# Layer 0, first pair of a two-layer directional scan: the upward scan's rows kept whole in DRAM, stored in 512-byte runs and loaded by columns in 128-byte runs

## The chip, the cores and the metric

The kernel runs on one core of a Trainium2 chip. The metric is device microseconds of one execution. All numbers are float32.

## The reference

A tensor x of 32 images, 48 channels, 64 rows and 128 columns goes through two layers. Each layer normalizes x by groups of three channels and then runs four scans, one after the other, over rows and then over columns; in each, a line becomes its own value plus a 5-tap convolution of the line before it.

```python
def _conv1d(x, w, b):                     # 48 -> 48 channels, 5 taps along the line
    y = conv_general_dilated(x, w, window_strides=(1,), padding=[(2, 2)], ...)
    return y + b[None, :, None]
def step(w, b):
    def f(carry, inp):
        nxt = inp + _conv1d(carry, w, b)
        return (nxt, nxt)
    return f
D = scan(step(down_w, down_b))  over rows 0..63
U = scan(step(down_w, down_b))  over D's rows 63..0
R = scan(step(right_w, right_b)) over U's columns 0..127
L = scan(step(left_w, left_b))  over R's columns 127..0
...
x = x + layer0(_gn(x));  x = x + layer1(_gn(x))      # _gn: group norm, 16 groups
```

A scan is serial: step n needs the line of step n-1. A row scan has 63 steps, a column scan 127.

## The kernel before

**Phases.** The 32 images are four groups of eight. `PHASES` sets the order: in layer 0, the rows of group 0, 1, 2 and 3 (phases 0 to 3, each a down scan and an up scan), then the columns of the first pair (groups 0 and 1, phase 4, a right scan and a left scan) and of the second pair (groups 2 and 3, phase 5); then the same for layer 1. The page names a step's PSUM tile `step_01d` for layer 0, group 1, down; `u` is up, and `step_00r` and `step_00l` are the right and left scans of layer 0, first pair. One step is 18 matmul records on TensorE (nine products, each split in two passes) and three `scalar_tensor_tensor` on VectorE (L913), one for each third of the partitions. VectorE's instruction of a step reads the PSUM sum, the bias and the line's own value, and writes the new line in place of that value; the next step's matmuls read it.

**Layouts.** In a row phase a partition holds one (column modulo 8, channel), 384 of them in three parts of 128, and its free axis holds the rows one after the other: a row is 128 floats, 16 columns by 8 images, 512 bytes. In a column phase a partition holds one (row modulo 8, channel); a quarter of the columns (`quarter`, j = 0 to 3) is six units of 128 x 2048 floats, 8 KB in a partition. Between the two the data go through DRAM. The tensors `upa` (one for each group, layer 0) keep the up scan's rows, `xin` keeps the input turned into the row layout, and `mid` the result of layer 0.

**Buffers.** `arena` has three slots of 48 KB in a partition and a stage of four units. A row phase takes two slots (rows 0 to 31 and rows 32 to 63), a column phase three: quarters 0, 1 and 2 lie in the three slots, and quarter 3 takes the place of quarter 0 after that has been spilled to DRAM.

**Queues.** Nearly all transfers of layer 0 are issued by SyncE (SP on the page) in program order (L288 for all, the helper `dma`). A DMA uses one of eight semaphores in turn, so a new one waits until the eighth before it has landed. `PIECES` cuts a block of 384 partitions into ten pieces of 48, 32 or 16 partitions: a block of eight rows is ten DMAs, a quarter of columns of two groups is twenty. What SP issues in phases 0 to 3, by the page's names:

- `arena<-in_x`: a part of the raw input of a later group, 2 MB, in six pieces for a group (`take_in`);
- `xin<-arena`: that input after GpSimd has turned it (L699, `permute`), 1 KB runs (`put_out`);
- `arena<-xin`: the rows of the next phase, in four loads of 16 rows, twenty DMAs each, 128-byte runs (`move_rows` with `to_dram` false);
- `upa<-arena`: the rows of an up scan, in eight stores of eight rows, ten DMAs each, 128-byte runs (`move_rows` with `to_dram` true, through `by_row`);
- `arena<-upa`: the quarters of the column phase, runs of 8 KB, one for each partition (`load_unit`, through `by_col`).

**Order.** `plan_rows`, `plan_cols` and `plan_input` give each piece of side work a time in steps, and all engines' instructions are written out in that order. For a row phase that starts at step t0, `plan_rows` puts the loads of rows 0, 16, 32 and 48 at t0-36, -26, 0 and +11 (phase 1: -34, -18, -3 and +12) and their scaling on ScalarE (L777, `scale_rows`, 24 instructions for 16 rows) at t0-18, -8, +16 and +30 (phase 1: -12, -2, +17 and +33). The stores of an up scan that starts at t_up stand at t_up+12, 20, 28 and 36 for rows 56 to 32, and for rows 24 to 0 at 30, 42, 54 and 66 steps into the next phase. `plan_input` puts the statistics of a later group's input on ScalarE between them (L570 and L562, `take_others`), one batch for each of the six `in_x` pieces; phase 1 does group 2's, phase 2 group 3's. After the sixth batch, VectorE makes the group's scale from them (L587 to L603) among the steps of the up scan. `plan_cols` loads quarter 0 at 54 to 44 steps ahead of the column phase, quarter 1 at 24 to 14 ahead, quarter 2 at 8 to 18 behind its start, the spill of quarter 0 at 33 to 43 and quarter 3 at 50 to 60.

The functions that the change touches and those that call them, with the line numbers of the profile:

Of the kernel before, what the change touches and what calls it, by code (L numbers as in the profile page):

```python
# [42 lines left out]
E8 = 8  # L43
FULL = 128
NG = E8 * C // FULL
NQ = 4
# [68 lines left out]
    ("cols", 1, 1),  # L115
)
JOINED = (8, 9)


@with_exitstack  # L120
def kernel(
# [11 lines left out]
    NH = H // E8  # L133
# [3 lines left out]
    RUN = KQ * GB  # L137
# [89 lines left out]
    def by_row(t, e, h0, h1):  # L227


        t = t.rearrange("c (i q a e n) -> e a c i q n", i=E8, q=NQ, a=NH, e=E8)[e, h0 // E8]  # L230
        t = t[:, h0 % E8 : h0 % E8 + h1 - h0]
        return t.rearrange("c i q n -> c (i q) n")

    def x_by_row(t, e, h0, h1):

        t = t.rearrange("(i q) c (a e n) -> e a c i q n", i=E8, a=NH, e=E8)[e, h0 // E8]
        return t[:, h0 % E8 : h0 % E8 + h1 - h0].rearrange("c i q n -> c (i q) n")
# [44 lines left out]
    def by_col(t, e, j):  # L282


        return t.rearrange("c (i q n) -> i q c n", i=E8, q=NQ)[e, j]

    def dma(dst, src, queue=None):
        (queue or nc.sync).dma_start(dst, src)  # L288
# [21 lines left out]
    def pieces(o):  # L310
        return [(e, c0, c1, p0) for e, c0, c1, g, p0 in PIECES if g == o]
# [404 lines left out]
    def place(k, h):  # L716


        first = k
        while first in JOINED:  # L720
            first -= 1
# [5 lines left out]
    def rows_at(k, h0, h1):  # L727

        places = sorted(place(k, h) for h in range(h0, h1, E8))
        at = places[0] * E8 + h0 % E8  # L730
        assert h0 // HALF == (h1 - 1) // HALF and places[-1] - places[0] == len(places) - 1
        return row_views(k)[h0 // HALF][:, :, at : at + h1 - h0]
# [4 lines left out]
    def move_rows(k, h0, h1, to_dram):  # L737

        _, layer, g = PHASES[k]
        t = (ups if to_dram else source)[layer][g]  # L740
        for h in range(h0, h1, E8):
            end = min(h1, h + E8)
            view = rows_at(k, h, end)
            for o in range(NG):
                for e, c0, c1, p0 in pieces(o):
                    here = view[p0 : p0 + c1 - c0, o]
                    here = here.rearrange("p h (q n) -> p (h q) n", q=NQ)
                    if to_dram:
                        dma(by_row(t, e, h, end)[c0:c1], here)
                    else:  # L750
                        dma(here, (x_by_row if g else natural_row)(t, e, h, end)[c0:c1])
# [41 lines left out]
    def quarter(k, j):  # L793
        return slot[slots(k)[j % 3]].rearrange("p (o s n) -> p s o n", s=2, o=NG)

    def load_unit(k, j, i):


        _, layer, pair = PHASES[k]
        o, half = UNITS[i]  # L800
        unit = quarter(k, j)[:, half, o]
        t = ups[layer][2 * pair + half]
        for e, c0, c1, p0 in pieces(o):
            here = unit[p0 : p0 + c1 - c0]
            dma(here, by_col(t, e, j)[c0:c1])

    def spill_unit(k, i, back):
        _, layer, pair = PHASES[k]
# [134 lines left out]
    def two_row_step(ku, hu, kd, hd):  # L943

        _, layer, g = PHASES[ku]
        first = slots(ku)[0] < slots(kd)[0]

        def both(u, d, o):
            u, d = lines(u[:, o]), lines(d[:, o])
            return beside(*((u, d) if first else (d, u)))  # L950

        def inp(o):
            if hu:
                return both(row(ku, hu - 1), row(kd, hd), o)
            pair = lines(last.rearrange("p (o n) -> p o n", o=NG)[:, o]), lines(row(kd, hd)[:, o])
            return pair if first else pair[::-1]

        def part(t, s):
            return t[:, max(0, s) : NK + min(0, s)]

        step(
            f"{layer}{g}u{hu}d{hd}",
            wt[f"down{layer}"],
            (layer, DOWN),
            lambda i: both(row(ku, hu + 1), row(kd, hd - 1), i),
            inp,
            lambda o: both(row(ku, hu), row(kd, hd), o),
            lambda ps: ps.rearrange("p (c q m b) -> p c q m b", c=2, q=NQ, b=GB),
            part,
            lambda t: t.rearrange("p c q m b -> p (q m) c b"),  # L970
        )
# [27 lines left out]
    def scans(k):  # L999
        if PHASES[k][0] == "rows":  # L1000
            if k not in JOINED:
                for h in range(1, H):
                    yield 1, lambda h=h: row_step(k, h, row(k, h - 1), row(k, h), "d")
            end = last.rearrange("p (o n) -> p o n", o=NG)
            for h in range(H - 2, -1, -1):
                if k + 1 in JOINED:
                    yield 2, lambda h=h: two_row_step(k, h, k + 1, H - 1 - h)
# [13 lines left out]
    def at(t, fn, *args):  # L1021
        agenda.append((t, len(agenda), fn, args))
# [31 lines left out]
    def plan_rows(k, t0, prev):  # L1054
        layer = PHASES[k][1]
        down, up = (2 if k in JOINED else 1), (2 if k + 1 in JOINED else 1)
        t_up = t0 + down * (H - 1)
# [4 lines left out]
        else:  # L1062
            ahead, scaled = (-54, -43, 0, 11), (-22, -8, 16, 30)
            if not PHASES[k][1]:
                ahead, scaled = (-36, -26, 0, 11), (-18, -8, 16, 30)
        if k in JOINED:
            for i in range(H // E8):
                h, t = i * E8, t0 + 2 * i * E8
                for o in range(NG):
                    at(t - 34 + 2 * o, take_rows, k, h, h + E8, o)  # L1070
                at(t - 17, scale_rows, k, h, h + E8)
        elif k:
            for i in range(4):
                if PHASES[k][1]:
                    for o in range(NG):
                        t = t0 + ahead[i] - 2 + 3 * o
                        at(t, take_rows, k, i * LOAD, (i + 1) * LOAD, o)
                else:
                    at(t0 + ahead[i], move_rows, k, i * LOAD, (i + 1) * LOAD, False)
                at(t0 + scaled[i], scale_rows, k, i * LOAD, (i + 1) * LOAD)  # L1080

        following = PHASES[k + 1][0] == "cols"
        for i in range(H // E8):
            h0 = H - E8 * (i + 1)
            t = t_up + up * (H - 1 - h0)
            if up == 2:
                t += 1
            elif not following and not layer:
                t = t_up + 12 + 8 * i if i < 4 else t_up + H - 1 + 30 + 12 * (i - 4)
            elif not following:  # L1090
                t = t_up + 29 + 5 * i + (34 if i >= 4 else 0)
            at(t, move_rows, k, h0, h0 + E8, True)
# [7 lines left out]
    def plan_cols(k, t0, prev):  # L1100
# [3 lines left out]
        for i in range(n):  # L1104
            early = 30 if after else 58 if k - 1 in JOINED else 54
            at(t0 - early + 2 * i, load_unit, k, 0, i)
            at(t0 + (3 if after else -24 + 2 * i), load_unit, k, 1, i)
            at(t0 + (38 if after else 8) + 2 * i, load_unit, k, 2, i)
            at(t0 + 33 + 2 * i, spill_unit, k, i, False)
            at(t0 + 50 + 2 * i, load_unit, k, 3, i)  # L1110
# [77 lines left out]
    starts, end = [], 0  # L1188
    for k, (kind, *_) in enumerate(PHASES):
        n = (H if kind == "rows" else W) - 1  # L1190
        starts.append(end - 2 * n if k in JOINED else end)
        end = starts[-1] + (2 if k in JOINED else 1) * n + (2 if k + 1 in JOINED else 1) * n
# [28 lines left out]
    def first_group():  # L1221
# [163 lines left out]
        scale_at_once(0, 2, 4, nc.vector)  # L1385
        put_rows(pool, act, pool)
        move_rows(0, 8, 12, False)
        put_rows(pool, act, pool, act, pool, act)
        scale_shared(8, 12)
# [84 lines left out]
```

## Time and profile before

| | us |
|---|---|
| median of 3 runs | 4126.9 (4126.24 to 4131.73) |
| profiled execution, its own time | 4129.7 |
| its span, first to last instruction | 4128.0 |
| TensorE busy | 4015.7 |
| VectorE busy | 2082.2 |
| ScalarE busy | 1307.0 |
| GpSimd busy | 789.3 |

The profiled execution lies 2.8 us above the median. TensorE's step starts place the phases, in us from the span's start: phase 0 down 61.3 and up 198.7; phase 1 down 324.5 and up 457.7; phase 2 down 586.8 and up 718.2; phase 3 down 845.7 and up 970.2; phase 4 right 1094.6 and left 1343.0; phase 5 from 1591.3; layer 1 from 2090.9. A row of the windows view gives a stretch of time, the busy time of each engine in it with its number of instructions, then the granted TensorE clock, the mean busy share of the 16 DMA engines and the GB/s that they moved. A row of the timeline gives the start, the length, the engine, the operation, out<-in, how many equal ones follow each other, and in brackets the idle time ahead of it and what ended that. For SP the length is the time in which it issued, not the time of the transfer.

### The profile page before, as it was taken

What the parts mean: (1) busy time and instruction counts of PE and PEld (TensorE: products, weight loads), DVE (VectorE), ACT (ScalarE), POOL (GpSimd) and SP (SyncE); (2) the same over time, 40 slices, a digit from 0 to 9 for tenths busy, and PEclk for the clock granted to TensorE, in tenths of its full rate; (3) what the DMA queues carried; (4) which work ended last, traced back from release to release, by engine and by line L of the source; (5) the groups of instructions that cost most, each with busy time, mean ns of one, the idle gap of its engine ahead of it and who ended that gap; (6) DMA issues with size and microseconds to landing.
All of it is one profiled execution on the core that took longest, in us unless ns stands there. A gap on an engine that the chain in (4) does not pass through costs nothing. (4 is left out here: it accounts for less than half of the span.)

```text
span 4128.0 us, 85199 instructions
## 1 busy us (share of the span) xinstructions
PE 4015.7 (97%) x34360; PEld 3930.1 (95%) x34360; DVE 2082.2 (50%) x6137; ACT 1307.0 (32%) x2628; POOL 789.3 (19%) x672
## 2 busy tenths in 40 slices
PE   6999999999999999999999999999999999999994
PEld 5999999999999999999999998888999999999994
DVE  6454454544444567545656443333444444444444
ACT  4556547450000256003674633434000002300122
POOL 5631303200000243002411000000000015610353
PEclk9999999999999999999999999999999999999997
DMA  9898998986990399814896965666698029999799
GB/s 300 217 203 171 222 157 211 208 132 116 165 226 1 89 261 285 210 20 151 217 171 146 141 107 95 100 108 100 100 171 205 1 70 252 294 246 157 148 233 195
DMA packets 2207818, 681.57 MB, mean 165 GB/s; under 512 B 2008848, under 2 KB 2157504, under 8 KB 2182080
## 3 DMA queue, kind: packets, MB, share of 16 engines
q1 hardware_dynamic: 2071488, 595.36, 69.7%
q10 hardware_dynamic: 135936, 80.77, 8.1%
q8 instruction: 270, 4.42, 0.5%
q14 instruction: 124, 1.02, 0.1%
HBM read 399.11 MB, written 295.93 MB: 168 GB/s over the span
## 5 line engine op out<-in xcount | busy, mean ns | idle before, releaser
L834 POOL TENSOR_TENSOR arena<-arena 128x2048 f32<-128x2048 f32 x80 | 362.5, 4548 | 1714.7 <-PE step_00l L899 499.9
L777 ACT ACTIVATE arena<-arena,offsetr,scaler 128x128 f32<-128x128 f32 (+1 forms) x576 | 345.1, 687 | 348.4 <-DMA arena<-mid 291.0
L638 ACT ACTIVATE early<-arena 128x256 f32<-128x256 f32 x192 | 129.7, 676 | 816.0 <-POOL arena L834 809.6
L777 ACT ACTIVATE arena<-arena,offset,scale 128x256 f32<-128x256 f32 (+2 forms) x360 | 248.8, 785 | 151.4 <-DMA arena<-xin 143.2
L699 POOL COPY arena<-arena 128x256 f32<-128x256 f32 x340 | 201.0, 658 | 443.1 <-DMA arena<-in_x 392.5
L899 PE MATMUL step_01r<-arena,early 128*128 128x128 f32 x2286 | 249.8, 272 | 0.0
L899 PE MATMUL step_11r<-arena,early 128*128 128x128 f32 x2286 | 249.3, 272 | 0.0
L899 PEld LDWEIGHTS step_11r<-arena,early 128*128 128x128 f32 x2286 | 248.7, 184 | 0.6 <-DVE arena L913 0.3
L899 PEld LDWEIGHTS step_01r<-arena,early 128*128 128x128 f32 x2286 | 248.9, 184 | 0.2
L899 PE MATMUL step_00r<-arena,early 128*128 128x128 f32 x2286 | 248.5, 272 | 0.0
L899 PE MATMUL step_10l<-arena,wleft 128*128 128x128 f32 x2286 | 248.5, 272 | 0.0
L899 PE MATMUL step_11l<-arena,wleft 128*128 128x128 f32 x2286 | 248.5, 272 | 0.0
L899 PE MATMUL step_10r<-arena,early 128*128 128x128 f32 x2286 | 248.5, 272 | 0.0
L899 PEld LDWEIGHTS step_00r<-arena,early 128*128 128x128 f32 x2286 | 248.5, 184 | 0.0
L899 PE MATMUL step_00l<-arena,wleft 128*128 128x128 f32 x2286 | 248.4, 272 | 0.0
L899 PE MATMUL step_01l<-arena,wleft 128*128 128x128 f32 x2286 | 248.4, 272 | 0.0
L899 PEld LDWEIGHTS step_10l<-arena,wleft 128*128 128x128 f32 x2286 | 248.4, 184 | 0.0
L899 PEld LDWEIGHTS step_11l<-arena,wleft 128*128 128x128 f32 x2286 | 248.4, 184 | 0.0
L899 PEld LDWEIGHTS step_10r<-arena,early 128*128 128x128 f32 x2286 | 248.4, 184 | 0.0
L899 PEld LDWEIGHTS step_00l<-arena,wleft 128*128 128x128 f32 x2286 | 248.4, 184 | 0.0
L899 PEld LDWEIGHTS step_01l<-arena,wleft 128*128 128x128 f32 x2286 | 248.4, 184 | 0.0
L856 ACT COPY arena<-arena 128x256 f32<-128x256 f32 x172 | 99.7, 657 | 367.1 <-POOL arena L834 241.0
(545 smaller groups left out, 6880.6 us busy)
## 6 DMA issues: line engine op xcount, KB each, us to landing
xin<-arena SPq DMA_DIRECT2D x94, 512.0 KB, 5.1
arena<-in_x SPq DMA_DIRECT2D x18, 2048.0 KB, 10.0
upa<-arena SPq DMA_DIRECT2D x192, 192.0 KB, 4.1
arena<-upa SPq DMA_DIRECT2D x96, 384.0 KB, 11.7
arena<-xin SPq DMA_DIRECT2D x96, 384.0 KB, 10.7
upb<-arena SPq DMA_DIRECT2D x192, 192.0 KB, 3.9
arena<-upb SPq DMA_DIRECT2D x96, 384.0 KB, 11.1
arena<-xin SPq DMA_DIRECT2D x174, 192.0 KB, 4.3
```

The source lines that it names most:

```text
L638: nc.scalar.activation(junk[:, 0:n], view[:, b], AF.Identity, accum_out=self.sum[:, i, j : j + 1])
L699: copy(dst[:, r, q], src[:, r0 + r, q])
L777: nc.scalar.activation(args[0], args[0], AF.Identity, bias=args[2], scale=args[1])
L834: eng.tensor_tensor(unit, unit, nat, ALU.add)
L856: copy(by_w(perm)[:, a], src[:, a])
L899: nc.tensor.matmul(part(turn(whole(ps[o]))[0:m], -s), weights[:, i, at : at + m], part(turn(src(i)), s), start=seen[o] == 1, stop=seen[o] ...
```

## The change

The DRAM tensors of layer 0's groups 0 and 1 are read as (channel, row modulo 8, row divided by 8, column modulo 8, 128 floats): the 16 columns by 8 images of one row and one column residue stand together, 512 bytes. Before, they stood in four runs of 128 bytes, one in each quarter of the columns. A store of eight rows now has 8 runs of 512 bytes for a partition in place of 32 of 128, and a load of a unit has 64 runs of 128 bytes for a partition, 512 bytes apart, in place of one of 8 KB. Groups 2 and 3 and layer 1 keep the old form.

```diff
 JOINED = (8, 9)
+WHOLE = ((0, 0), (0, 1))
...
+    def whole_row(t, e, h0, h1):
+        t = t.rearrange("c (i a e n) -> e a c i n", i=E8, a=NH, e=E8)[e, h0 // E8]
+        return t[:, h0 % E8 : h0 % E8 + h1 - h0]
...
+    def part_of_rows(t, e, j):
+        return t.rearrange("c (i m q n) -> i q c m n", i=E8, q=NQ, n=RUN)[e, j]
...
                 for e, c0, c1, p0 in pieces(o):
                     here = view[p0 : p0 + c1 - c0, o]
+                    if to_dram and (layer, g) in WHOLE:
+                        dma(whole_row(t, e, h, end)[c0:c1], here)
+                        continue
                     here = here.rearrange("p h (q n) -> p (h q) n", q=NQ)
...
-            dma(here, by_col(t, e, j)[c0:c1])
+            if (layer, 2 * pair + half) in WHOLE:
+                dma(here.rearrange("p (m n) -> p m n", n=RUN), part_of_rows(t, e, j)[c0:c1])
+            else:
+                dma(here, by_col(t, e, j)[c0:c1])
```

Of 320 stores to `upa` 160 change their form, and of 160 loads from it 80. No instruction is added, removed or moved on any engine. A row of SP's list gives its number, the line, out<-in and the sizes of the destination: partitions, runs, floats of a run. The first store of group 0's up scan read before:

```order
78 L288 DMA upa_88<-arena 48x32x32 x2
79 L288 DMA upa_88<-arena 32x32x32
80 L288 DMA upa_88<-arena 16x32x32
81 L288 DMA upa_88<-arena 48x32x32 x2
82 L288 DMA upa_88<-arena 16x32x32
```

and now (the helper `dma` has moved from L288 to L298):

```order
78 L298 DMA upa_88<-arena 48x8x128 x2
79 L298 DMA upa_88<-arena 32x8x128
80 L298 DMA upa_88<-arena 16x8x128
81 L298 DMA upa_88<-arena 48x8x128 x2
82 L298 DMA upa_88<-arena 16x8x128
```

Nothing moved: a partition's eight rows go out in 8 runs of 128 floats, where they went in 32 runs of 32. The first loads of phase 4 on the same list read before:

```order
520 L288 DMA arena<-upa_88 48x2048 x2
521 L288 DMA arena<-upa_88 32x2048
522 L288 DMA arena<-upa_89 48x2048 x2
523 L288 DMA arena<-upa_89 32x2048
524 L288 DMA arena<-upa_88 16x2048
```

and now:

```order
520 L298 DMA arena<-upa_88 48x64x32 x2
521 L298 DMA arena<-upa_88 32x64x32
522 L298 DMA arena<-upa_89 48x64x32 x2
523 L298 DMA arena<-upa_89 32x64x32
524 L298 DMA arena<-upa_88 16x64x32
```

They stand at the same places, and a partition's unit comes in 64 runs of 32 floats, where it came in one of 2048.

## Prediction

> **What bounds the kernel now.** I read the waits of TensorE first, since a chain of serial steps ends when TensorE's last step ends; each row gives who waited for whom, us in total, times, longest.
>
> ```profile
> PE step_01d L899 <- DVE arena L913: 6.8, 1, 6.8
> PE step_02d L899 <- DVE arena L913: 5.4, 1, 5.4
> PE step_01u L899 <- DVE arena L913: 2.8, 3, 1.5
> PE step_02u L899 <- DVE arena L913: 1.5, 2, 1.3
> ```
>
> Apart from the first 170 us, which the change doesn't reach, TensorE waits in phases 1 and 2 and nowhere else for more than a fraction of a microsecond. The windows view, cut at the starts of the scans (phase 0 up; 1 down, up; 2 down, up; 3 down, up), prices it.
>
> ```profile
> 198.70:324.50 125.80, 125.55 (x1144) 125.36 (x1143) 63.81 (x211) 65.63 (x144) 40.41 (x69) 1.00 0.95 205
> 324.50:457.70 133.20, 126.36 (x1136) 126.17 (x1136) 60.73 (x190) 88.85 (x173) 32.17 (x55) 0.97 0.84 189
> 457.70:586.80 129.10, 126.33 (x1145) 125.76 (x1145) 65.48 (x211) 52.39 (x116) 25.46 (x44) 1.00 0.96 192
> 586.80:718.20 131.40, 126.00 (x1136) 125.81 (x1135) 60.64 (x189) 93.91 (x180) 31.43 (x54) 0.99 0.90 198
> 718.20:845.70 127.50, 125.95 (x1144) 125.57 (x1144) 65.84 (x211) 52.76 (x116) 27.88 (x46) 1.00 0.98 195
> 845.70:970.20 124.50, 124.50 (x1137) 124.50 (x1137) 60.57 (x190) 53.82 (x72) 0.00 (x0) 1.00 0.74 116
> 970.20:1094.60 124.40, 124.40 (x1136) 124.40 (x1135) 60.64 (x189) 0.00 (x0) 0.50 (x1) 1.00 0.89 150
> ```
>
> A quiet down scan takes 124.5 us (phase 3). An up scan in which VectorE also makes a group's scale takes 125.8 when nothing is late (phase 0). So phase 1 loses 8.7 and 3.3 us, phase 2 loses 6.9 and 1.7: 20.6 us in all. The granted clock is down to 0.97 and 0.99 just where TensorE stood still. Who is late is told by VectorE's and ScalarE's timelines and by the one line of source L588.
>
> ```profile
> 426.23 0.61 DVE L913 SCALAR_TENSOR_TENSOR arena<-step_01d,bd,arena 128x128 f32<-128x128 f32 x2 [7.10 <-DMA arena<-in_x]
> 655.33 0.61 DVE L913 SCALAR_TENSOR_TENSOR arena<-step_02d,bd,arena 128x128 f32<-128x128 f32 x2 [5.66 <-ACT arena L777]
> 525.16 0.21 DVE L592 TENSOR_TENSOR neg_x_x<-neg_x_x,mean_x_x 128x48 f32<-128x48 f32 x1 [2.56 <-ACT early L562]
> L588 DVE TENSOR_SCALAR mean_x_x<-mean_x_x x3: 171/1933/2222, 254.7 to 780.2; 128x8 f32<-128x8 f32 x3
> 512.11 9.48 POOL L699 COPY arena<-arena 128x256 f32<-128x256 f32 x16 [23.94 <-DMA arena<-in_x]
> ```
> ```profile
> 395.43 0.63 ACT L570 ACTIVATE early<-arena 128x512 f32<-128x512 f32 x1 [9.83 <-DMA arena<-in_x]
> 408.37 17.83 ACT L777 ACTIVATE arena<-arena,offset,scale 128x256 f32<-128x256 f32 x24
> 624.52 0.63 ACT L570 ACTIVATE early<-arena 128x512 f32<-128x512 f32 x1 [18.71 <-DMA arena<-in_x]
> 637.47 17.84 ACT L777 ACTIVATE arena<-arena,offset,scale 128x256 f32<-128x256 f32 x24
> ```
>
> VectorE stood 7.10 us ahead of row 48 of phase 1 and went on at 426.23, when the 24 scalings of rows 48 to 63 ended (408.37 + 17.83 = 426.20); the DMA named there landed long before. These scalings stand behind a batch of statistics, and that batch began when its piece of `in_x` landed (395.43). At 655.33 it is the same chain one batch earlier: `in_x`, statistics, rows 32 to 47. At 525.16 VectorE itself waits for the last batch. And L588, 0.17 us when alone, took 1.93 while GpSimd's copies ran to 521.59. All four are one lateness, that of the `in_x` pieces, and SP's timeline tells where they stand.
>
> ```profile
> 225.20 10.23 SPq L288 DMA_DIRECT2D upa<-arena  x10
> 239.83 12.74 SPq L288 DMA_DIRECT2D upa<-arena  x10
> 256.42 12.52 SPq L288 DMA_DIRECT2D upa<-arena  x10
> 289.89 11.10 SPq L288 DMA_DIRECT2D upa<-arena  x10
> 301.04 43.97 SPq L288 DMA_DIRECT2D arena<-xin  x40
> 345.06 0.98 SPq L288 DMA_DIRECT2D arena<-in_x  x1
> 383.94 1.00 SPq L288 DMA_DIRECT2D arena<-in_x  x1
> 615.07 1.31 SPq L288 DMA_DIRECT2D arena<-in_x  x1
> 616.43 26.27 SPq L288 DMA_DIRECT2D arena<-xin  x20
> ```
>
> SP issues without a pause from 225 to 346: four stores of group 0, then sixty row loads, then `in_x`. The queue is the bound there, not the step that a plan gives a transfer.
>
> **The stores.** Their price is read from stretches in which one kind of transfer runs (last two columns: busy share of the DMA engines, GB/s).
>
> ```profile
> 209.00:224.00 15.00, 15.00 (x139) 15.00 (x138) 7.17 (x24) 14.36 (x39) 13.60 (x24) 1.00 0.85 296
> 227.00:235.00 8.00, 8.00 (x76) 8.00 (x75) 3.85 (x12) 7.68 (x21) 6.80 (x12) 1.00 0.96 155
> 303.00:345.00 42.00, 42.00 (x384) 42.00 (x384) 20.57 (x64) 18.18 (x25) 0.00 (x0) 1.00 0.94 144
> 1137.00:1157.00 20.00, 20.00 (x186) 20.00 (x185) 10.06 (x32) 0.00 (x0) 0.00 (x0) 1.00 1.02 194
> 1206.00:1222.00 16.00, 16.00 (x150) 16.00 (x149) 7.87 (x26) 0.00 (x0) 0.00 (x0) 1.00 1.06 218
> ```
>
> They are: 1 KB runs stored from 128 partitions; 128-byte stores; 128-byte row loads; the 8 KB column loads; 1 KB and 8 KB loads of residuals in pieces of 48, 32 and 16 partitions. A block of eight rows is 384 x 4 KB = 1.57 MB. At 155 GB/s that is 10.1 us, which is the row 10.23. No row shows runs of 512 bytes. The ends: at 296/0.85 = 348 GB/s it takes 4.5 us, with no gain 10.2; a loss I leave out, since there are four times fewer runs of the same bytes. The nearest rows are those of the same pieces with long runs, 194 and 218. I take 200 GB/s: 7.9 us, a gain of 2.3 for a block.
>
> The four stores of phase 0 put SP 4 x 2.3 = 9.2 us ahead at the loads of 301.04 and so at 345.06 and 383.94. The rows that they store are ready in time (the fourth block at 198.7 + 31 x 1.98 = 260). Then rows 48 to 63 are scaled 9.2 us earlier, and the wait of 7.10 is gone by 2. The next bound there is the step itself. The eight stores between 345 and 615 give 18 more. On the way SP also waits for GpSimd and for its input buffer, which come free earlier by the same chain, so I count 20 to 27 of lead at 615.07. Phase 2 starts 8.7 + 3.3 = 12.0 earlier; its rows 32 need 12.0 + 5.66 = 17.7 of lead, its rows 48 (scaled just in time now) about 20. Both are met, the second with little to spare. With a lead of some 17 at the last batch, VectorE's 2.56 us is gone and GpSimd's copies end before L588 (521.59 - 17 against 519.7 - 8.7). In phase 2's up scan the lead is larger. So all 20.6 us come back. The price at which the first wait would remain: a block over 8.4 us.
>
> That the queue carries the same number of DMAs, ten for a block, is no new bound: ten row loads with fewer bytes are issued in less than 10 us, and the landing of eight in flight only gets quicker.
>
> **The loads.** These lie beside phases 3 and 4, whose TensorE is full. The rows: SP's issues of quarters 1 (its end), 2 and 3; the median time to landing of these 384 KB DMAs, 11.7 us; and the right scan's matmuls (first and last start).
>
> ```profile
> 1103.47 3.02 SPq L288 DMA_DIRECT2D arena<-upa  x6
> 1134.27 23.71 SPq L288 DMA_DIRECT2D arena<-upa  x20
> 1172.08 28.60 SPq L288 DMA_DIRECT2D arena<-upa  x20
> ```
> ```profile
> arena<-upa SPq DMA_DIRECT2D x96, 384.0 KB, 11.7
> ```
> ```profile
> L899 PE MATMUL step_00r<-arena,early x2286: 259/275/335, 1094.6 to 1342.9; 128*128 128x128 f32 x128, 128*96 128x112 f32 x63
> ```
>
> A step takes (1342.9 - 1094.6)/127 = 1.955 us, so quarter 1 is needed at 1094.6 + 31 steps = 1155, quarter 2 at 1218, quarter 3 at 1280. They landed at 1118, 1170 and 1212: 37, 48 and 68 us to spare. A quarter is 6.29 MB: 32.4 us at 194 GB/s. In 128-byte runs the same bytes are the forty row loads of 43.97 us, with the same partition pieces and as many runs: 44.0. Each quarter costs 11.6 more, and since DMA engines are full from 993 on, the delays add up: 23 at quarter 1, 35 at quarter 2, 46 at quarter 3. All are below what is to spare, the least by 13. The sum's term is 0; the cover is gone at a quarter of 48.4 us. The ends: 44.0, and the slowest 128-byte row loads, 26.27 for half a quarter beside a 2 MB `in_x`, 52.5: quarter 3 then lands 80 late against 68, 12 us of stall. I take 44.0, as no `in_x` runs there. Above these rows lies one thing that no row shows: runs 512 bytes apart, so that a quarter reads a fourth of each row. What is behind (residual loads, used from step 34 of the left scan) has over 100 us.
>
> Against this speaks a sum of fixed costs: 128-byte stores at 155 GB/s take 13.2 ns a run on each of 16 engines, 1 KB stores at 348 take 47.1, which leaves 8.4 ns for a run whatever its size. If that came on top of a quarter's 32.4, its 49152 runs would add 25.8 and make 58. The forty row loads are as many runs in the same pieces and took 44.0, so the two costs overlap, in those loads at least.
>
> The Trainium skill, DMA: Bandwidth & Descriptors, "Why small descriptors are slow (HBM only)", gives each packet about 3 cycles beside its 32-byte beats. By that rule, as an estimate, 64 runs of 128 bytes are 448 cycles where one of 8 KB is 259, and a quarter of 32.4 becomes 56 us, near the 58; the row of 43.97 doesn't bear it out for row loads.
>
> **Sum.** 4129.7 for the profiled execution less 20.6 is 4109.1. It stood 2.8 above the median, so 4126.9 - 20.6 = 4106.3 for the median.
>
> **Rivals.** First, a part only: a block costs over 8.4 us, say 9.2. Lead 4 at 383.94: phase 1 keeps 3 of its 7 us, phase 2's rows 48 some of theirs; 10 to 14 us come back, about 4115. For it: the stores stand among 1 KB stores (12.74, 12.52), where I priced them alone. Against: 194 and 218 in the same pieces.
>
> Second, slower: the cost of a run adds to the pace of the pieces, 58 us a quarter. That is 25.4 over the present; quarter 3 lands 102 later against 68 to spare, 34 us of stall, 4140. The point from which this decides: 20.6 = 4 x excess - 68, an excess of 22, a quarter of 54.6 us. Against it the 144 GB/s of the row loads, which would have to fall to 108. The skill's rule above would give 56 us and 4133.
>
> Third, slower too, by another cause: runs 512 bytes apart load at well under the row loads' rate. The long runs of these column loads go at 194 where 348 is seen elsewhere; the same fall would make 79 us of 44. Half way, 62 us: quarter 3 is 4 x 29.6 = 118 late, 50 of stall, 4157. Against: the fall is seen with residuals from another tensor (218), so it belongs to the pieces, which the 43.97 has already.
>
> Fourth, 512-byte runs gain nothing and the loads are hidden: 4127.
>
> **Chances.** All back: 0.63. A part: 0.16. Costs that add: 0.07. Runs apart: 0.06. Nothing: 0.08. Faster by over 0.2% (8.3 us, about what a measurement here can tell) is all back and nearly all of the part, 0.77; within 0.2% the nothing and the tail of the part, 0.10; slower 0.13. The range: the low end is the whole excess of phases 1 and 2 over phase 3 (8.7 + 4.7 + 6.9 + 3.1 = 23.4), with no cost of the scale left: 4103. The high end takes in the part: 4121. Left out are both slower ones and most of the nothing.
>
> **What would show it.** Right: no wait of TensorE over 2 us in phases 1 and 2; down scans of 124 to 126 us; the four stores under 9 us each; `in_x` issued near 336; quarter loads of twenty at about 44 us and none awaited; phase 4 at 248.3. Wrong: stores of 10 us, a new wait in `step_00r` near its steps 32, 64 or 96, or rows still scaled late because statistics and not SP set the pace.

## Result: 21.7 us faster, and the profile after

On one chip the kernel before took 4129.31 us (median of 4, 4126.24 to 4132.28), the changed one 4107.58 (median of 4, 4105.10 to 4109.53): a ratio of 0.9947 [0.9930, 0.9964], a gain of 15 to 29 us by its interval. The profiled execution of the changed kernel took 4108.49 of its own, its span is 4106.8, 21.2 below the 4128.0 of before. The line numbers have moved: `dma` is L298, TensorE's step L915, VectorE's L929, the statistics L580, the scaling L790.

The waits of TensorE after, from phase 0's up scan to phase 3 (us in total, times, longest). There are no others in these scans; `step_01d` and `step_02d` are gone from the list.

```profile
PE step_02u L915 <- DVE arena L929: 0.3, 1, 0.3
PE step_00u L915 <- DVE arena L929: 0.3, 1, 0.3
PE step_01u L915 <- DVE arena L929: 0.3, 1, 0.3
```

The windows after, cut again at the starts of the scans (phase 0 up; 1 down, up; 2 down, up; the last row is phase 4 right):

```profile
198.20:324.00 125.80, 125.55 (x1144) 125.36 (x1143) 63.87 (x211) 79.04 (x162) 40.34 (x69) 1.00 0.94 220
324.00:448.50 124.50, 124.50 (x1136) 124.50 (x1136) 60.60 (x190) 85.11 (x179) 38.27 (x65) 1.00 0.80 211
448.50:574.40 125.90, 125.65 (x1144) 125.46 (x1144) 63.91 (x211) 61.70 (x117) 19.52 (x33) 1.00 0.91 203
574.40:698.90 124.50, 124.50 (x1137) 124.50 (x1137) 60.62 (x190) 89.14 (x190) 37.93 (x64) 1.00 0.84 230
698.90:824.80 125.90, 125.64 (x1145) 125.45 (x1144) 63.96 (x211) 57.63 (x107) 21.38 (x35) 1.00 0.91 169
1073.60:1322.30 248.70, 248.70 (x2288) 248.47 (x2288) 122.30 (x382) 0.00 (x0) 0.00 (x0) 1.00 0.86 131
```

The four scans lost 8.7, 3.2, 6.9 and 1.6 us (133.2, 129.1, 131.4 and 127.5 before), 20.4 together, and each is now within 0.1 us of the length that a quiet scan of its kind had before (124.5 down, 125.8 up). The granted clock is 1.00 in all of them. Phase 4's right scan, in which the loads are slower, kept its length (248.7 here, 248.4 before, from 1094.6 to 1343.0).

SP's timeline after, rows 1 to 4 the four stores of group 0's up scan, then the row loads, the `in_x` pieces and the quarters of phase 4:

```profile
224.79 7.30 SPq L298 DMA_DIRECT2D upa<-arena  x10
236.07 9.23 SPq L298 DMA_DIRECT2D upa<-arena  x10
249.28 9.48 SPq L298 DMA_DIRECT2D upa<-arena  x10
279.10 7.84 SPq L298 DMA_DIRECT2D upa<-arena  x10
286.99 44.39 SPq L298 DMA_DIRECT2D arena<-xin  x40
331.44 0.63 SPq L298 DMA_DIRECT2D arena<-in_x  x1
370.15 0.87 SPq L298 DMA_DIRECT2D arena<-in_x  x1
576.09 0.83 SPq L298 DMA_DIRECT2D arena<-in_x  x1
1102.37 12.92 SPq L298 DMA_DIRECT2D arena<-upa  x6
1137.25 44.10 SPq L298 DMA_DIRECT2D arena<-upa  x20
1188.86 54.33 SPq L298 DMA_DIRECT2D arena<-upa  x20
```

The four stores take 33.9 us where they took 46.6, the row loads behind them are issued at the same pace as before (44.39 and 43.97), and so `in_x` is issued 13.6 us earlier. The quarters pay for it: quarter 2 was issued in 23.71 and takes 44.10, quarter 3 in 28.60 and takes 54.33.

Four rows of ScalarE's timeline after show where the lead arrives, and the line of VectorE's small scale instruction (L588 before; least, median and longest in ns) shows its stretch beside GpSimd's copies gone:

```profile
381.04 0.63 ACT L580 ACTIVATE early<-arena 128x512 f32<-128x512 f32 x1 [9.20 <-DMA arena<-in_x]
393.97 17.96 ACT L790 ACTIVATE arena<-arena,offset,scale 128x256 f32<-128x256 f32 x24
598.20 17.93 ACT L790 ACTIVATE arena<-arena,offset,scale 128x256 f32<-128x256 f32 x24
631.77 17.93 ACT L790 ACTIVATE arena<-arena,offset,scale 128x256 f32<-128x256 f32 x24
```
```profile
L598 DVE TENSOR_SCALAR mean_x_x<-mean_x_x x3: 171/171/171, 254.2 to 760.8; 128x8 f32<-128x8 f32 x3
```

Rows 48 to 63 of phase 1 are scaled at 393.97 + 17.96 = 411.9, and the step that needs them comes at 324.0 + 47 x 1.98 = 417.1: 5 us to spare where 7.1 were missing. Rows 32 to 47 of phase 2 are ready at 616.1 for a step at 574.4 + 31 x 1.98 = 635.8, and its rows 48 to 63 at 649.7 for a step at 667.5. From its issue (370.15) to the first statistic that reads it (381.04) the second `in_x` piece took 10.9 us, and 11.5 before (383.94 to 395.43): of the 14 us by which it is there earlier, the travel gives 0.6 and the issue the rest.

### The profile page after: what moved, and what is told of

It reads as the page before. It is cut to its first block, busy times and chain, and to the rows that moved or that the text cites. A ratio compares the mean times of both kernels' runs of the same rounds, so it can differ in the third digit from the quotient of the medians.

```text
span 4106.8 us, 85201 instructions
## 1 busy us (share of the span) xinstructions
PE 4012.3 (98%) x34360; PEld 3927.0 (96%) x34360; DVE 2078.8 (51%) x6137; ACT 1306.9 (32%) x2628; POOL 789.0 (19%) x672
## 5 line engine op out<-in xcount | busy, mean ns | idle before, releaser
L790 ACT ACTIVATE arena<-arena,offsetr,scaler 128x128 f32<-128x128 f32 (+1 forms) x576 | 345.2, 688 | 348.8 <-DMA arena<-mid 322.5
L790 ACT ACTIVATE arena<-arena,offset,scale 128x256 f32<-128x256 f32 (+2 forms) x360 | 249.0, 787 | 91.8 <-DMA arena<-xin 81.6
L915 PE MATMUL step_01r<-arena,early 128*128 128x128 f32 x2286 | 249.8, 272 | 0.0
L915 PE MATMUL step_11r<-arena,early 128*128 128x128 f32 x2286 | 249.2, 272 | 0.0
L915 PEld LDWEIGHTS step_11r<-arena,early 128*128 128x128 f32 x2286 | 248.7, 184 | 0.4 <-DVE arena L929 0.3
L915 PEld LDWEIGHTS step_01r<-arena,early 128*128 128x128 f32 x2286 | 248.9, 184 | 0.2
L915 PE MATMUL step_00r<-arena,early 128*128 128x128 f32 x2286 | 248.8, 272 | 0.0
L915 PEld LDWEIGHTS step_00r<-arena,early 128*128 128x128 f32 x2286 | 248.5, 184 | 0.2 <-DVE arena L929 0.2
L915 PE MATMUL step_10l<-arena,wleft 128*128 128x128 f32 x2286 | 248.5, 272 | 0.0
L915 PE MATMUL step_11l<-arena,wleft 128*128 128x128 f32 x2286 | 248.5, 272 | 0.0
L915 PE MATMUL step_00l<-arena,wleft 128*128 128x128 f32 x2286 | 248.4, 272 | 0.0
L915 PE MATMUL step_01l<-arena,wleft 128*128 128x128 f32 x2286 | 248.4, 272 | 0.0
L915 PE MATMUL step_10r<-arena,early 128*128 128x128 f32 x2286 | 248.4, 272 | 0.0
L915 PEld LDWEIGHTS step_10l<-arena,wleft 128*128 128x128 f32 x2286 | 248.4, 184 | 0.0
L915 PEld LDWEIGHTS step_11l<-arena,wleft 128*128 128x128 f32 x2286 | 248.4, 184 | 0.0
L915 PEld LDWEIGHTS step_00l<-arena,wleft 128*128 128x128 f32 x2286 | 248.4, 184 | 0.0
L915 PEld LDWEIGHTS step_01l<-arena,wleft 128*128 128x128 f32 x2286 | 248.4, 184 | 0.0
L915 PEld LDWEIGHTS step_10r<-arena,early 128*128 128x128 f32 x2286 | 248.4, 184 | 0.0
## 6 DMA issues: line engine op xcount, KB each, us to landing
arena<-in_x SPq DMA_DIRECT2D x18, 2048.0 KB, 10.5
arena<-upb SPq DMA_DIRECT2D x96, 384.0 KB, 10.9
```

The lines of the kernel that those rows point to most:

```text
L790: nc.scalar.activation(args[0], args[0], AF.Identity, bias=args[2], scale=args[1])
L915: nc.tensor.matmul(part(turn(whole(ps[o]))[0:m], -s), weights[:, i, at : at + m], part(turn(src(i)), s), start=seen[o] == 1, stop=seen[o] ...
```

## The experiments

The theory: the 128-byte stores made SP's in-order queue late, everything behind it inherited this (`in_x`, the statistics, the scaling, VectorE's step), and 512-byte stores undo it, while the slower loads are hidden by 10 to 15 us. The rivals: the loads pay or gain something of their own; ScalarE's order of work and not SP sets the pace; the loads are hidden by far more than worked out, so that their price would not matter. In the diffs, minus is the changed kernel (for the third experiment the kernel before).

**The stores alone.**

```diff
-            if (layer, 2 * pair + half) in WHOLE:
+            if False:                       # load_unit: 8 KB runs for all groups
```

> Stores of groups 0 and 1 in 512-byte runs as in the changed kernel, but phase 4 loads its units as before, one run of 8 KB for a partition; the columns so loaded are in another order, and the output is not the reference's. Theory (the gain is SyncE's queue, which the shorter stores put ahead; the loads of phase 4 are hidden): the same time as the changed kernel, 4106 to 4109 us, 0.995 of before. Rival (the loads cost something that the stores pay back): faster than the changed kernel by over 4 us, 4103 or less.

Measured: 4106.8 us against 4127.25, a ratio of 0.9951 [0.9939, 0.9964]. That is the changed kernel's time, so the whole gain is the stores', and the slow form of 80 loads costs nothing that is seen here.

**The loads alone.**

```diff
-                    if to_dram and (layer, g) in WHOLE:
+                    if False:               # move_rows: 128-byte stores for all groups
```

> Stores as before in 128-byte runs, loads of phase 4 in 64 runs of 128 bytes, 512 bytes apart, as in the changed kernel; the data so loaded are in another order, and the output is not the reference's. Theory: no gain and no loss, 4126 to 4132 us, all waits of phases 1 and 2 as before; a quarter of twenty DMAs takes 44 us to issue and lands 10 us or more ahead of its first use. Rival (the loads have a cost): slower by over 4 us, with a wait of TensorE in the right scan of phase 4.

Measured: 4126.06 against 4127.25, 0.9999 [0.9991, 1.0008]. The waits of TensorE with the loads alone are nearly those of the kernel before in phase 1 and in phase 2's down scan, and there is none of `step_00r`. In phase 2's up scan 1.5 us were expected and 0.3 are left; no load of the new form stands ahead of that scan, so I take it for a difference between executions, as it is seen with group 1 below.

```profile
PE step_01d L915 <- DVE arena L929: 6.0, 1, 6.0
PE step_02d L915 <- DVE arena L929: 5.2, 1, 5.2
PE step_01u L915 <- DVE arena L929: 1.5, 2, 1.2
```

SP issues quarter 2 here in 47.53 us, against 23.71 in the kernel before, and nobody notices:

```profile
1156.40 47.53 SPq L298 DMA_DIRECT2D arena<-upa  x20
```

**ScalarE's order, in the kernel before.** Rows 48 to 63 (phase 1) and 32 to 63 (phases 2 and 3) are scaled before the batch of statistics that stood ahead of them. If the order on ScalarE set the pace, the gain would be had without touching a store.

```diff
-            ahead, scaled = (-34, -18, -3, 12), (-12, -2, 17, 33)
+            ahead, scaled = (-34, -18, -3, 12), (-12, -2, 17, 22)
-                ahead, scaled = (-36, -26, 0, 11), (-18, -8, 16, 30)
+                ahead, scaled = (-36, -26, 0, 11), (-18, -8, 7, 22)
```

> The kernel before, with ScalarE's scaling of rows 48 to 63 of phase 1 and of rows 32 to 63 of phase 2 written ahead of the batch of statistics that they stood behind. Theory (SyncE's queue sets when the in_x pieces land, and the last batch of statistics bounds the up scan): the waits at row 48 and row 32 go, but VectorE then waits for the last batch by as much more, about 11 us in phase 1's up scan and 7 in phase 2's; the time stays, 4124 to 4130 us. Rival (the order on ScalarE alone is the cause): 15 us faster, 4112.

Measured: 4130.02 against 4128.6, 1.0002 [0.9993, 1.0011]. The windows of this kernel (phase 1 down, up; phase 2 down, up) and its waits of TensorE:

```profile
323.80:448.30 124.50, 124.50 (x1137) 124.50 (x1135) 60.45 (x189) 85.22 (x164) 28.77 (x49) 1.00 0.82 184
448.30:585.70 137.40, 128.56 (x1145) 128.11 (x1144) 66.72 (x211) 57.77 (x127) 28.73 (x49) 0.96 0.97 198
585.70:710.10 124.40, 124.40 (x1137) 124.40 (x1136) 60.42 (x189) 88.99 (x169) 28.46 (x48) 1.00 0.88 196
710.10:848.00 137.90, 128.88 (x1145) 128.50 (x1144) 68.97 (x211) 60.24 (x131) 30.78 (x51) 0.96 0.98 194
```
```profile
PE step_02u L899 <- DVE arena L913: 9.0, 2, 8.8
PE step_01u L899 <- DVE arena L913: 8.8, 2, 8.6
```

The down scans are quiet at once, as quiet as with the long stores, and the up scans lose 11.6 and 12.1: the last batch of statistics now comes late for the group's scale, because its `in_x` piece still stands at its old place in SP's queue. ScalarE begins that batch at 510.40, when the piece lands (512.09 in the kernel before, whose up scan began 9.4 us later). VectorE's timeline has it as an instruction that waits for ScalarE, and the next one stretched from 0.17 to 3.09 us beside GpSimd's copies, which waited for the same piece (510.43 to 519.74):

```profile
510.40 0.63 ACT L570 ACTIVATE early<-arena 128x512 f32<-128x512 f32 x1 [20.08 <-DMA arena<-in_x]
516.44 0.20 DVE L587 TENSOR_REDUCE mean_x_x<-sum_x_x 128x8 f32<-128x48 f32 x1 [6.33 <-ACT early L570]
516.67 3.09 DVE L588 TENSOR_SCALAR mean_x_x<-mean_x_x 128x8 f32<-128x8 f32 x1
```

So the order on ScalarE decides only where the lateness is paid; SP's pace sets how much.

**One group at a time.** Four of group 0's eight stores stand ahead of phase 1's first `in_x`, the other four and four of group 1's between that and phase 2's first.

```diff
-WHOLE = ((0, 0), (0, 1))
+WHOLE = ((0, 0),)
```

> The new form for group 0 alone. Theory: the stores of phase 0 and of phase 1's first half set the lead, so phase 1 is freed wholly and phase 2's down scan too (the lead at its first in_x is 27 us where 20 are needed); only phase 2's up scan keeps its 1.7: 4107 to 4111 us. Rival (the gain goes with the number of short runs taken away, half the stores, half the gain): 4118.

Measured: 4109.63, 0.9955 [0.9943, 0.9968]. All four scans are free (124.7, 126.1, 124.6 and 126.1 us); the 1.7 us of phase 2's up scan that I expected to stay did not. The last of the four:

```profile
699.80:825.90 126.10, 125.85 (x1146) 125.66 (x1145) 63.88 (x211) 51.08 (x102) 21.46 (x35) 1.00 0.97 182
```

Group 0's eight stores, four in phase 0 and four in phase 1, are enough: phase 2's first `in_x` is issued at 584.30, 30.8 us ahead of the kernel before (39.0 with both groups).

```diff
-WHOLE = ((0, 0), (0, 1))
+WHOLE = ((0, 1),)
```

> The new form for group 1 alone. Theory: nothing changes ahead of group 1's first store at 468 us, so the 7.1 us wait at row 48 of phase 1 stays whole; phase 1's up scan gains about 3, phase 2 its 6.9 and 1.7: 4115 to 4120 us. Rival (the gain goes with the number of short runs taken away): also 4118, but then with the wait of phase 1 shortened to half.

Measured: 4117.25, 0.9975 [0.9965, 0.9985], the time that was expected. The profile did not fit it at first: the wait ahead of row 48 in phase 1, which group 1's stores can't touch, was 0.7 us and not 7.

```profile
PE step_01d L915 <- DVE arena L929: 0.7, 1, 0.7
```

In that execution the `in_x` piece landed at 391.6 (395.4 before) and the phase began at 326.9 (324.5 before), and both shorten the wait. Nor did phase 1's up scan gain the 3 us that were expected: it lost 1.1 more than before.

```profile
452.50:582.70 130.20, 127.75 (x1144) 127.15 (x1143) 66.63 (x211) 64.03 (x136) 28.85 (x49) 0.99 0.92 204
```

To see whether the form of group 1 shortened the wait, the same kernel ran once more:

> The new form for group 1 alone, once more: its first profile had a wait of only 0.7 us at row 48 of phase 1, where the theory said 7. The theory's own terms give that wait: the end of the 24 scalings less the time at which the scan reaches row 48, both as the profile has them. In that first profile phase 1 began 2.4 us later than before and the in_x piece landed 3.8 us earlier, 6.2 together. If those two wander from one execution to the next, another execution has a wait between 0 and 8 us and a time that goes with it; if group 1's form shortened it, the wait is under 1 again with phase 1 begun near 324.5.

It took 4117.7, with the wait back, the piece landing at 396.8 and the phase beginning at 327.2:

```profile
PE step_01d L915 <- DVE arena L929: 5.7, 1, 5.7
```

The wait wanders by 5 us from one execution to the next, with the piece's issue (381.76 in the first, 385.42 in the second). One trace gives its size no better than that. What it leaves out at row 48 comes back in large part in the up scan: in the first execution phase 1's two scans took 125.6 and 130.2 us, in the second 132.5 and 125.9, together 2.6 apart.

**Runs of 256 bytes.** Rows are stored in two halves, and loaded again in 128-byte runs.

```diff
...
-        return t[:, h0 % E8 : h0 % E8 + h1 - h0]             # 8 runs of 128 floats
+        t = t[:, h0 % E8 : h0 % E8 + h1 - h0]                # 16 runs of 64 floats
+        return t.rearrange("c i s n -> c (i s) n")
...
```

> Groups 0 and 1 kept with halves of rows together: stored in runs of 256 bytes, loaded in 128-byte runs 256 bytes apart. By runs, between 10.23 us (12288 runs) and 7.31 (3072), a block of 6144 costs about 8.3. Theory: the lead at 345 us is then about 8 us, the wait at row 48 is just gone or down to 1, phase 2 is freed but for its rows 48: 4107 to 4114 us. Rival (only runs of 512 bytes or more gain): 4125 or more.

Measured: 4108.96, 0.9953 [0.9940, 0.9967]; no wait is left in phases 1 and 2. The first store is in between:

```profile
226.26 8.63 SPq L300 DMA_DIRECT2D upa<-arena  x10
```

10.23, 8.63 and 7.30 us for 128, 256 and 512 bytes. A little over half of the saving on a block already buys the whole gain, since what counts is only to be ahead of the step.

**Using up the slack.** In phase 4, four of quarter 2's six units are loaded a second time, into the stage, among the real ones.

```diff
...                                      # load_extra: the same DMAs as load_unit, into the stage
+            if k == 4 and i < 4:
+                at(t0 + 7 + 2 * i, load_extra, k, i)
```

> The changed kernel with four units of quarter 2 loaded a second time into the stage, between the loads of quarter 2: 4/6 of a quarter of 44 us, 29.3 us more. In the changed kernel quarter 2 landed at 1186.5 and was needed at 1196.9. Theory (SyncE's queue and the DMA engines are the bound there, the loads are hidden by 10 us only): TensorE waits about 19 us ahead of step 64 of the right scan, 4126 to 4127 us. Rival (more slack than this reading says): 4108 to 4112.

Measured: 4126.12 against 4128.6, 0.9994 [0.9986, 1.0003], the expected time. SP's row for quarter 2, VectorE's step that waited, and TensorE's wait (this profile is of the quickest execution, 4119.99):

```profile
1132.34 75.02 SPq L298 DMA_DIRECT2D arena<-upa  x34
```
```profile
1210.95 0.61 DVE L936 SCALAR_TENSOR_TENSOR arena<-step_00r,bd,arena 128x128 f32<-128x128 f32 x2 [13.19 <-DMA arena<-upa]
```
```profile
PE step_00r L922 <- DVE arena L936: 12.9, 1, 12.9
```

30.9 us more of issue (75.02 less 44.10) cost 18.5 by the medians, so some 12 were to spare. In the profile shown the issue ends 26.0 us later than in the changed kernel's (1207.36 and 1181.35) and TensorE waits 12.9, which gives 13. The column loads do have a price, and it lies 12 us below the surface.

**All four groups.** If the stores of groups 2 and 3 are priced as those of 0 and 1, and their loads lie beside phases 4 and 5 with the same slack, nothing should be lost.

```diff
-WHOLE = ((0, 0), (0, 1))
+WHOLE = ((0, 0), (0, 1), (0, 2), (0, 3))
```

> The new form for all four groups of layer 0. Theory: phases 2 and 3 have no waits left that stores could shorten, so there is no gain; the second pair's column loads cost 11 us a quarter more beside the residual loads and the result's stores of phases 4 and 5, with 18 to 24 us to spare: 4106 to 4118 us, a wait in phase 5's right scan if any. Rival (the stores' time itself is on the path): 4097 or less.

A miss: 4147.84 against 4128.6, 1.0049 [1.0036, 1.0062], some 40 us above the changed kernel. SP's timeline at the start of phase 5, GpSimd's and VectorE's next instructions, and TensorE's wait:

```profile
1595.21 48.31 SPq L298 DMA_DIRECT2D arena<-upa  x20
1643.62 2.55 SPq L298 DMA_DIRECT2D arena<-xin  x3
```
```profile
1653.09 4.49 POOL L850 TENSOR_TENSOR arena<-arena 128x2048 f32<-128x2048 f32 x1 [48.15 <-DMA arena<-xin]
1657.62 0.62 DVE L625 BATCH_NORM_STATS2 bn_r<-arena 128x6 f32<-128x256 f32 x1 [35.34 <-POOL arena L850]
```
```profile
PE step_01r L915 <- DVE arena L929: 37.5, 3, 34.7
```

No wait for the column loads shows here, but only because TensorE already stood: their issue ended at 1643.5, and step 31 of a scan that began at 1570.4 would have needed them at 1631. Behind them in the queue stand the loads of the first pair's residuals. The changed kernel's rows at this place, with phase 5 beginning at the same time (1570.6 there, 1570.4 here):

```profile
1571.91 25.73 SPq L298 DMA_DIRECT2D arena<-upa  x20
1599.35 2.89 SPq L298 DMA_DIRECT2D arena<-xin  x3
```

The residuals' loads follow at 1599.35 there and at 1643.62 here. GpSimd's addition waits for them, VectorE's statistics wait for GpSimd, and they stand on VectorE ahead of a step. I had counted 11 us more for a quarter. Quarter 1 took 22.6 more (48.31 and 25.73) and began 23.3 later (1595.21 and 1571.91), and the slack of what stands behind it I had not counted at all.

**All four groups, with residuals first.** The same, and quarter 1 of phase 5 is issued eight steps later, behind the first two residual loads.

```diff
+            late = 11 if k == 5 else 3
-            at(t0 + (3 if after else -24 + 2 * i), load_unit, k, 1, i)
+            at(t0 + (late if after else -24 + 2 * i), load_unit, k, 1, i)
```

> All four groups in the new form, with the two residual loads of phase 5 written ahead of quarter 1's twenty column loads, not behind them. Theory (with all groups VectorE's statistics waited 35 us for GpSimd's addition, and that for a residual load held up behind 48 us of column loads): that wait is gone; but quarter 1 now starts when the last residual's buffer is free, near 1606, takes 48 and lands near 1659, where step 32 needs it at 1631: a wait of TensorE of about 28 us, 4135 us. Rival (the order of the residual loads was the only fault): 4108 to 4118.

Measured: 4147.59 against 4125.77, 1.0051 [1.0034, 1.0067], 12 more than expected. The wait for the residuals is gone, and the step now waits for the quarters:

```profile
DVE arena L929 <- DMA arena<-upa: 33.1, 2, 20.1
```
```profile
1598.41 49.98 SPq L298 DMA_DIRECT2D arena<-upa  x20
```

One wait of 19.9 us is at 1632, where quarter 1 is first needed; I expected 28. The second, 12.7 us, is further on in the scan: quarter 2, behind a queue that is still late, which I had not foreseen. In both orders what was put last was late; at the pace of 44 to 50 us a quarter there is no room here for the short loads of a second pair in either of the two orders tried.

## Why the prediction was right

- **Which resource.** That the short stores cause all four losses, by way of late `in_x` pieces, is shown: the stores alone give the whole gain, ScalarE's order gives none, and the pieces gain in their issue and not in their travel. One thing is not separated: while the short stores run, the DMA engines are busy too (0.96), and no run issued `in_x` ahead of the stores or from another queue. Whether the place in SP's queue alone would do stays open.
- **The price of a block.** Taken as 7.9 us from the nearest rows (between 4.5 and 10.2); the first block measures 7.30. But two of the four measure 9.23 and 9.48, above the 9 that was named as a sign of being right, and the mean is 8.5, above the 8.4 at which the first wait was to remain. It went all the same, because these blocks had cost 12.5 to 12.7 before and not 10.2: the saving counts, and the rival of 9.2 a block falls by its lead, 13.6 where it had 4.
- **The lead.** 4 x 2.3 = 9.2 us predicted, 13.6 measured. The step that was mis-sized: I used the price of a block alone for all four, but the blocks that stand among `xin` stores shrank as much or more, from 12.74 to 9.23, 12.52 to 9.48 and 11.10 to 7.84. Together the four give 12.7. At the third `in_x` row (615.07 before, 576.09 after) the lead is 39.0 where 20 to 27 were predicted. Both count the 12.0 to 12.4 us by which phase 2 itself starts earlier, so this term too was too small. The eight stores between 345 and 615 were to give 18; they took 107.4 us before and 69.6 after, 37.7 less, and SP's waits for GpSimd took back some of it (32.1 us before, 46.0 after). The last two of the eight, before and after:

```profile
548.83 20.71 SPq L288 DMA_DIRECT2D upa<-arena  x20
517.31 14.21 SPq L298 DMA_DIRECT2D upa<-arena  x20
```

- **The waits.** All gone, with 5 us to spare at row 48 of phase 1, where 2 were predicted. For phase 2 rows 48 were to have "little to spare"; they had 17.8 us, and rows 32 had 19.7, since the lead was so much larger. The errors of the two terms lay on the safe side: the waits would have gone with the predicted lead as well, by its own sums.
- **The loads.** 44.0 us a quarter predicted, 44.10 measured for quarter 2, so the costs of a run and of the pieces overlap here too, and runs 512 bytes apart are no slower than the row loads. The two dearer rivals fall (costs that add, 58 us; runs apart, 62): no wait for a quarter is left. The 348 GB/s that the third rival calls seen elsewhere is 296 divided by a busy share, not a rate in a row. Quarter 3 measured 54.33, above the upper end that I gave, 52.5, and the work beside it is another than I named there. Its first 10 us of issue share the DMA engines with the spill of quarter 0, which I had left out. The match of quarter 2 is no fixed price either: with the loads alone it took 47.53.
- **The slack.** The last DMA of quarter 1 landed at 1119.2 for a step at 1134, that of quarter 2 at 1186.4 for one at 1196.9, that of quarter 3 at 1246.7 for one at 1259.5: 15, 10.5 and 13 us. I had 14, 13 and 22. The least was right within 3 us, and the loading experiment gives 12 or 13; quarter 3's was too large by 9, for the reason just given.
- **The sum.** 20.6 predicted, 21.7 between the medians and 20.4 in the four scans. The time alone would not tell 20.6 from 15 or 29 (its interval); the four scans do. The 4107.58 is 1.3 above the 4106.3, as the median of before is 4129.31 with a fourth execution, where it was 4126.9 with three, and the gain is 1.1 larger.

The Trainium skill, DMA: Bandwidth & Descriptors, "Why small descriptors are slow (HBM only)", would have given 56 us for a quarter by its cycles for each packet, an estimate from the 32.4 us of the long runs, or 112 GB/s. The trace does not agree, at 44.10 in the row at 1137.25 and 137 GB/s from 1141 to 1180.

## What to carry to other kernels

Price a transfer by its place in an in-order queue: a store that nobody waits for cost 20 us here, because work with a due time stood behind it, and a slower load cost nothing, because 10 us were left behind it. In all the forms tried here short runs were left on one of the two sides of the transposition through DRAM; put them where the queue has slack, and count the slack of everything behind them too (the same form for two more groups lost 40 us that way). When a wait goes away after a reordering, look for the next one behind the same queue before you count it as a gain.

## What was not expected of the hardware

- The time of a block is not in proportion to the number of runs: 12288, 6144 and 3072 runs take 10.23, 8.63 and 7.30 us for the same 1.57 MB.
- Loads of 128-byte runs that stand 512 bytes apart go at about the pace of row loads: 44.10 and 43.97 us for 6.29 MB, though other rows of twenty such loads took 47.53 to 54.33.
- The same wait, in the same kernel, was 0.7 us in one execution and 5.7 in another, with a time that differed by 2.6 us between them (4115.13 and 4117.7).
- VectorE's 128x8 instruction, 0.17 us when alone, took 3.09 and 5.18 us beside GpSimd's work in the experiment on ScalarE's order, and 1.93 and 2.22 before the change. Only the timing beside GpSimd is shown, not the reason.
